# Two of a group's four normalised inputs turned by DMA transposes through DRAM, and the last group's input prepared a slot sooner

## The chip, the cores and the metric

The kernel runs on one core of a Trainium2 chip. The metric is the device time of one execution in microseconds. One execution per kernel is also taken by the hardware profiler, and all views shown here come from such an execution. The engines are called as the profile calls them: PE is the matrix engine and PEld its weight loads, DVE the vector engine, ACT the scalar engine, POOL the GpSimd engine, SP the queue from which this kernel issues all its DMAs.

## The reference

Two layers are applied to `x`, 128 graphs of 128 nodes with 512 features each, in float32.

```
h = relu(layernorm(x));  x = x + norm_adj @ (h @ W0) + b0
h = relu(layernorm(x));  q, k, v = h@Wq+bq, h@Wk+bk, h@Wv+bv        (8 heads of 64)
attn = softmax(q k^T / 8 + (1 - adj) * -1e9);  x = x + (attn @ v) @ Wo + bo
```

`norm_adj` and the mask come from one 128x128 matrix that all graphs share. All the large products are 512x512 weights against 512 rows of a group.

## The kernel before, in words

**Groups and slots.** Four graphs ("elements" 0 to 3) make a group, and there are NG = 32 groups. `xts[g, half]` holds the residual of two elements, 128 nodes by 2 x 512. The program is a sequence of slots t = 0 to 32, and each slot has the stages W, Q, K, V and Y, in this order. W is the first layer's weight product for group t+1, Q, K and V are the projections of group t, and Y is the output projection of group t-1. So a group's first layer runs a slot before its projections, and its output projection is in the same slot, after V.

**Stages and places.** A stage is a 512x512x512 product cut into 2x2 blocks, computed by seven block products instead of eight (class `Projection`, steps n = 0 to 6), and most block products are cut in the same way once more. What a step leaves for later (`tail`) runs in steps 1 and 2 of the stage that follows. All other work is hung on the steps by name: `at(t, "V2", f, ...)` puts a call ahead of step 2 of stage V in slot t, `"V2b"` puts it between the two parts of that step. `block` (L991) walks the steps and calls what the plan holds. The order on each engine is this written order; no scheduler moves anything. "V2" is called a place below.

**Operands.** The left operand of a stage is a tile of 40 slots of 128x128 float32 (class `Operands`). Slots 0 to 15 hold the blocks A11, A12, S1 and A22. The transposed input of elements 0 and 1 goes into A11 and A12 (slots 0 to 7), that of elements 2 and 3 into S1 and A22 (slots 8 to 15). `combine` then makes the sums that the seven products need, four operations over 512 columns and nine over 256, on POOL in most slots. There are three such tiles: `op_mix` (`op_a`, input of W), `op_norm` (`op_h`, input of Q, K and V) and `op_att` (`op_o`, input of Y).

**How the input of Q, K and V is made.** In slot t, for group g = t+1: `ln2` (DVE, then POOL) makes mean and scale, `norm_h` (L662, ACT) writes the normalised element `h` [128 nodes, 512 features], `transpose_h` (L666) turns it by four PE transposes into a small PSUM bank and copies the bank into `op_norm` (L673, ACT). Then `attention_operands` (L675) is the `combine`. `norm_h` stands at V5, V6, Y1 and Y2, `transpose_h` at Y1, Y2, Y3 and Y4, and `attention_operands` at Y5. Q of the next slot reads the result.

**How the softmaxed scores are turned.** These 124 tiles are already turned by DMA. `split_att` (L771) has ACT copy the float32 tile, seen as 16-bit halves, into two planes (all low halves, then all high halves), in a tile of `att_buf` that is free, and SP writes the planes to DRAM. `turn_att` (L777) has SP issue a DMA transpose of the planes back into SBUF, which puts the halves side by side again. `att_buf` has five tiles for the four elements of a group, and `att_of(g, b)` is tile (b - g) mod 5. In slot t these steps belong to group t-1, and `attend` at V0 reads their results; group 31 is turned on PE instead (`transpose_att`).

**The SP queue.** All DMAs stand in one queue in written order, and an entry that waits holds up those behind it. In a slot there are the reloads of the weights (`reload_w`, L966: of each weight four parts, into two buffers in turn, each as soon as the stage that read the buffer is past that part), four plane writes, four DMA transposes, two loads of `x` for group t+2 (`load_x`, at W3 and W5) and two stores of finished halves (`store_half`: one after Y, one at W3). A load of `x` goes into a tile whose store must have landed first. In DVE's order, the statistics of the loaded `x` (`ln1`, at Q0b) stand between reads of PE's banks.

**The end.** In slot 31 there is no W, so the chain that prepares Q and the attention of group 30 has no stage beside it.

Of the kernel before, what the change touches and what calls it, by code (L numbers as in the profile page):

```python
# [9 lines left out]
U16 = mybir.dt.uint16  # L10
# [16 lines left out]
A11, A12, S1, A22, S2, S3, S4 = range(7)  # L27
# [17 lines left out]
LEFT_AT = {A11: 0, A12: 4, S1: 8, A22: 12, S2: 16, S3: 20, S4: 24}  # L45
# [48 lines left out]
def kernel(  # L94
# [16 lines left out]
    nc = tc.nc  # L111
    B, N, D = x.shape
    P = 128
    H = 8
    HD = D // H
    NC = D // P
    GB = 4
    NG = B // GB
# [27 lines left out]


    planes_dram = [dp.tile([P, 2, H * P], U16, tag=f"planes_{b}", name=f"planes_{b}") for b in range(GB)]
    adj_sb, an = (att_buf[2][:, i, :] for i in range(2))
    bias_part = att_buf[4][:, 0:NC, :].rearrange("p c f -> p (c f)")  # L150
    ones = att_buf[4][:, NC, :]
# [430 lines left out]
    hs = {}  # L582
# [82 lines left out]

    def transpose_h(g, b):  # L666
        if b == 0:
            op_h[g] = op_norm
        h2 = hs.pop((g, b))
        pt = small_bank(f"pt_{g}_{b}")  # L670
        for c in range(NC):
            nc.tensor.transpose(pt[:, c * P : (c + 1) * P], h2[:, c * P : (c + 1) * P], ident)  # L672
        nc.scalar.copy(op_h[g].blocks_of(b), pt.rearrange("p (c n) -> p c n", c=NC))  # L673

    def attention_operands(g):  # L675
        op_h[g].combine(nc.vector if g < 2 else nc.gpsimd, g > 0, within=nc.gpsimd)
# [42 lines left out]
    def att_of(g, b):  # L719


        return att_buf[(b - g) % (GB + 1)]
# [65 lines left out]

    def attend(g, b):
        if g not in op_o:  # L790

            op_o[g] = op_mix if g == NG - 1 else op_att
        aT = att_of(g, b if g == NG - 1 else b - 1)
        if b == 2 or b == 3:
            po = small_bank(f"po_{g}_{b}")
        else:
            po = bank["b" if b == 0 else f"a{1 - turn[0]}"]
        for c in range(NC):
            for p in range(2):
                h = 2 * c + p  # L800
                nc.tensor.matmul(  # L801
                    po[p * HD : (p + 1) * HD, c * P : (c + 1) * P],
                    vs[g][:, b, h * HD : (h + 1) * HD],
                    aT[:, p * NC + c, :],
                    start=True,
                    stop=True,
                )
        nc.scalar.copy(op_o[g].blocks_of(b), po.rearrange("p (c n) -> p c n", c=NC))
# [17 lines left out]
    def at(slot, place, f, *args):  # L826
        plan.setdefault((slot, place), []).append((f, *args))

    for t in range(-1, NG + 1):


        last = t == NG - 1
        if 0 <= t - 1 < NG - 1:
            g = t - 1
            for place, first, f, *args in (
                ("Q0", "W1", turn_att, 0),
                ("W1b", "W4b", split_att, 1),
                ("W2", "W5", exponentials, 2, 0, H // 2),
                ("W3", "W6", exponentials, 2, H // 2, H),
                ("W4b", "Q0b", softmax_end, 2),  # L840
                ("W5", "Q1", exponentials, 3, 0, H // 2),
                ("W6", "Q2", exponentials, 3, H // 2, H),
                ("Q2", "Q0", turn_att, 1),
                ("Q0b", "Q2b", softmax_end, 3),
                ("Q3b", "Q4b", split_att, 2),
                ("Q5b", "Q6b", split_att, 3),
                ("K0", "K1", turn_att, 2),
                ("K2", "K3", turn_att, 3),
            ):
                at(t, place if t > 1 else first, f, g, *args)  # L850
            for b in (2, 3, 0, 1):
                at(t, "V0", attend, g, b)
        if t == 0:

            at(0, "Q0b", ln2, 1, 0)
            at(0, "Q1b", ln2, 1, 1)
            at(0, "K6", norm_h, 1, 0)
            at(0, "K6", norm_h, 1, 1)
            at(1, "W0", transpose_h, 1, 0)
            at(1, "W0", norm_h, 1, 2)  # L860
            at(1, "W1", transpose_h, 1, 1)
            at(1, "W1", norm_h, 1, 3)
            at(1, "W2", transpose_h, 1, 2)
            at(1, "W3", transpose_h, 1, 3)
            at(1, "W3", attention_operands, 1)
            at(2, "W6", attention_residual, 1, 0)
            at(2, "W6", attention_residual, 1, 1)
        elif 1 <= t + 1 < NG and t >= 0:
            g = t + 1
            at(t, "K0b", ln2, g, 0)  # L870
            at(t, "K3b", ln2, g, 1)
            at(t, "V5", norm_h, g, 0)
            at(t, "V6", norm_h, g, 1)
            at(t, "Y1", transpose_h, g, 0)
            at(t, "Y1", norm_h, g, 2)
            at(t, "Y2", transpose_h, g, 1)
            at(t, "Y2", norm_h, g, 3)
            at(t, "Y3", transpose_h, g, 2)
            at(t, "Y4", transpose_h, g, 3)
            at(t, "Y5", attention_operands, g)  # L880
            at(t + 1, "Q3", attention_residual, g, 0)
            at(t + 1, "Q4", attention_residual, g, 1)
        if 1 < t <= NG:

            at(t, "Y3" if t == NG else "Q3" if last else "W3", store_half, t - 2, 1)
        if 3 <= t + 2 < NG:
            at(t, "W3" if t > 1 else "W0", load_x, t + 2, (0,))
            at(t, "W5" if t > 1 else "W0", load_x, t + 2, (1,))
        if 2 <= t + 2 < NG:
            g = t + 2  # L890
            at(t, "Q0b", ln1, g, 0, (0,), ())
            at(t, "Q1b", ln1, g, 0, (1,), (0, 1))
            at(t, "Q3b", ln1, g, 1)
            places = (("Q3", "Q5"), ("Q4", "Q6"), ("Q5b", "K1"), ("Q6", "K2"))
            for b, (norm, mix) in enumerate(places):
                at(t, norm, gcn_norm, g, b)
                at(t, mix, gcn_mix, g, b)
            at(t, "K2" if t > 0 else "V1b", gcn_operands, g)
            at(t, "Y1" if t > 0 else "K3", gcn_residual, g, 0)
            at(t, "Y2" if t > 0 else "K3", gcn_residual, g, 1)  # L900
        if 0 <= t < NG:
            g = t
            for b in (0, 1, 3, 2):
                at(t, "V0", scores, g, b)
            if t > 0:
                at(t, "V0", output_operands, t - 1)
            at(t, "V1b", row_max, g, 0)
            at(t, "V3b", exponentials, g, 0, 0, H // 2)
            at(t, "V4b", exponentials, g, 0, H // 2, H)
            at(t, "V6", softmax_end, g, 0)  # L910
            if last:
                at(t, "V5b", row_max, g, 1)
                at(t, "V5b", exponentials, g, 1, 0, H // 2)
                at(t, "V6", exponentials, g, 1, H // 2, H)
                at(t, "Y1b", softmax_end, g, 1)
                at(t, "Y2", transpose_att, g, 0)
                at(t, "Y4", transpose_att, g, 1)
            else:
                if t > 0:
                    at(t, "V3b", row_max, g, 1)  # L920
                    at(t, "Y1", exponentials, g, 1, 0, H // 2)
                    at(t, "Y2", exponentials, g, 1, H // 2, H)
                    at(t, "Y4", softmax_end, g, 1)
                else:
                    at(t, "V4b", row_max, g, 1)
                    at(t, "V5b", exponentials, g, 1, 0, H // 2)
                    at(t, "V6", exponentials, g, 1, H // 2, H)
                    at(t + 1, "W1b", softmax_end, g, 1)
                at(t, "Y3b", split_att, g, 0)
                at(t, "V6b", row_max, g, 2)  # L930
                at(*((t, "Y1") if t > 0 else (1, "W0")), add_mask, g, 3)
                at(*((t, "Y6b") if t > 0 else (1, "W4b")), row_max, g, 3)
        if last:
            g = t
            at(t, "Y0", row_max, g, 2)

            at(t + 1, "W0", combine_w, "o last", nc.gpsimd)
            at(t, "Y1", exponentials, g, 2, 0, H)
            at(t, "Y1b", row_max, g, 3)
            at(t, "Y2b", softmax_end, g, 2)  # L940
            at(t, "Y3", exponentials, g, 3, 0, H)
            at(t, "Y4b", softmax_end, g, 3)
            at(t, "Y6", transpose_att, g, 2)
            at(t + 1, "W0", transpose_att, g, 3)
            for b in range(GB):
                at(t + 1, "W0", attend, g, b)
            at(t + 1, "W0", output_operands, g)

            at(t + 1, "Y4", store_half, g, 0, slice(0, 256))
            at(t + 1, "Y5", store_half, g, 0, slice(256, 512))  # L950
            at(t + 1, "Y6", store_half, g, 1, slice(256, 512))
# [191 lines left out]
```

## Time and profile before

| what | value |
|---|---|
| time, median of 3 runs | 2330.02 us (2326.16 to 2332.68) |
| time of the profiled execution | 2329.11 us |
| its span, first to last instruction | 2327.3 us |
| granted TensorE clock, mean | 0.997 |
| DVE busy | 1869.4 us (80%) |
| ACT busy | 1344.8 us (58%) |
| POOL busy | 1861.7 us (80%) |
| DMA queue, share of 16 engines' span | 74.9% |

Busy times are unions of the instructions' spans on an engine. A slot in the middle takes some 71 us: the scores of V0 start at 1007.11 us in slot 13 and at 1078.46 us in slot 14. The end of slot 13 and the start of slot 14 are used as the example throughout: V0 from 1003.46, the V product from 1010.88 and Y from 1021.88 us in slot 13, W from 1035.06, Q from 1046.77 and K from 1060.65 us in slot 14.

### The profile page before, as it was taken

The numbers are of one execution on the slowest core, as the hardware profiler recorded it, in microseconds if no ns is written. First come the engines' busy times: TensorE is split into PE (matmuls) and PEld (weight loads), VectorE is DVE, ScalarE is ACT, GpSimd is POOL, SyncE is SP. The second block draws the span as 40 slices with busy tenths as digits, with TensorE's granted clock in tenths as the row PEclk, the third lists the DMA queues.
The fourth block names the chain that finished last, engine by engine and source line by source line (L and its number), as shares of the span: only waits on it lengthen the run. The fifth ranks groups of instructions, "written<-read, shape, count | busy, mean of one in ns | idle before, by whom it ended". The sixth has DMA issues, their size and how long they took to land.

```text
span 2327.3 us, 50893 instructions
## 1 busy us (share of the span) xinstructions
PE 2300.2 (99%) x18359; PEld 2155.6 (93%) x18359; DVE 1869.4 (80%) x4832; ACT 1344.8 (58%) x3553; POOL 1861.7 (80%) x1927
## 2 busy tenths in 40 slices
PE   8999999999999999999999999999999999999999
PEld 8889999999999999999999999999999999999988
DVE  6777888788888788887888878888878888888866
ACT  3555665655656556556566565565655665655564
POOL 6898788878788777887778887778877788877764
PEclk9999999999999999999999999999999999999999
DMA  6388877789767788777887678886788877788873
GB/s 199 126 257 247 252 227 232 214 247 276 226 228 217 238 252 248 234 226 216 250 267 225 229 213 249 254 242 227 221 226 257 270 217 230 216 247 259 233 217 104
DMA packets 390764, 536.07 MB, mean 230 GB/s; under 512 B 271856, under 2 KB 279152, under 8 KB 390000
## 3 DMA queue, kind: packets, MB, share of 16 engines
q1 hardware_dynamic: 390512, 532.81, 74.9%
q8 instruction: 146, 2.39, 0.4%
q14 instruction: 106, 0.87, 0.1%
HBM read 358.68 MB, written 109.05 MB: 201 GB/s over the span
## 4 chain that ended last, share of the span: by engine, by line
PE 82%; DMA 5%; DVE 5%; issue 1%; POOL 0%; SPq 0%; ACT 0%; DVEq 0%; ACTq 0%
PE bank_a L387 30%; PE bank_d L387 18%; PE bank_b L387 9%; PE bank_c L387 9%; DMA xt<-in_x_dram 5%; PE pa L604 4%; PE bank_d L734 3%; PE po L801 3%; PE pt L672 2%; DVE xt L428 2%; PE pss L734 1%; DVE xt L438 1%; PE bank_b L801 1%; PE bank_a L801 1%; PE bank_b L734 1%
## 5 line engine op out<-in xcount | busy, mean ns | idle before, releaser
L761 ACT ACTIVATE att<-att,nmx 128x128 f32<-128x128 f32 x1024 | 396.0, 389 | 0.6 <-DVE nmx L753 0.5
L387 PE MATMUL bank_a<-op_h,w 128*128 128x256 f32 x1536 | 364.6, 380 | 0.0
L769 POOL TENSOR_TENSOR att<-att,rsm 128x1024 f32<-128x1024 f32 x128 | 242.8, 1897 | 100.0 <-DVE rsm L768 98.1
L387 PEld LDWEIGHTS bank_a<-op_h,w 128*128 128x128 f32 x1536 | 278.6, 191 | 30.3
L428 DVE TENSOR_TENSOR xt<-xt,bank_d 128x512 f32<-128x512 f32 x732 | 269.1, 416 | 25.9 <-PE bank_d L387 9.0
L332 ACT ACTIVATE h<-xt,nb,rs 128x512 f32<-128x512 f32 x254 | 206.9, 816 | 71.4 <-POOL nb L321 69.7
L319 POOL TENSOR_TENSOR rs<-ve,mhalf 128x2 f32<-128x2 f32 (+1 forms) x129 | 91.3, 708 | 193.3 <-DVE ve L318 193.0
L695 ACT ACTIVATE q<-bank_a,bqk 128x256 f32<-128x256 f32 x192 | 80.6, 470 | 285.7 <-PE bank_a L387 285.7
L774 ACT COPY att<-att 128x2048 uint16<-128x2048 uint16 x124 | 235.4, 1899 | 7.2 <-POOL att L769 7.2
L387 PE MATMUL bank_d<-op_h,w 128*128 128x128 f32 (+1 forms) x1768 | 225.5, 279 | 3.9 <-POOL op_h L90 3.1
L387 PEld LDWEIGHTS bank_d<-op_h,w 128*128 128x128 f32 x1768 | 210.7, 192 | 9.1 <-issue 4.0
L90 POOL TENSOR_TENSOR op_o<-op_o 128x256 f32<-128x256 f32 x297 | 209.3, 729 | 10.0
L90 POOL TENSOR_TENSOR op_h<-op_h 128x256 f32<-128x256 f32 x279 | 196.7, 730 | 13.5 <-DVE op_h L364 3.8
L90 POOL TENSOR_TENSOR op_a<-op_a 128x256 f32<-128x256 f32 x270 | 190.4, 728 | 14.7 <-DVE op_a L364 5.3
L313 DVE BATCH_NORM_STATS2 st<-xt 128x6 f32<-128x512 f32 x256 | 173.2, 676 | 24.8 <-DMA xt<-in_x_dram 24.8
L761 ACT ACTIVATION_READ_ACCUMULATOR att<-att,nmx 128x1 f32 x1024 | 192.8, 188 | 0.0
L438 DVE TENSOR_TENSOR xt<-bank_a,xt 128x512 f32<-128x512 f32 x252 | 167.4, 686 | 18.4 <-PE bank_a L387 10.8
L387 PE MATMUL bank_a<-w,op_o 128*128 128x256 f32 x768 | 181.7, 379 | 0.0
L387 PE MATMUL bank_a<-w,op_h 128*128 128x256 f32 x744 | 179.1, 384 | 0.0
L387 PE MATMUL bank_a<-w,op_a 128*128 128x256 f32 x744 | 176.8, 381 | 0.2 <-DVE xt L438 0.2
L741 DVE SCALAR_TENSOR_TENSOR att<-bank_d,msk 128x512 f32<-128x512 f32 x128 | 82.5, 686 | 104.8 <-PE bank_d L734 96.2
L753 DVE TENSOR_REDUCE nmx<-att 128x8 f32<-128x1024 f32 x128 | 155.0, 1211 | 0.0
(178 smaller groups left out, 5937.8 us busy)
## 6 DMA issues: line engine op xcount, KB each, us to landing
w<-wd_v SPq DMA_DIRECT2D x93, 704.0 KB, 5.6
w<-wd_o SPq DMA_DIRECT2D x93, 704.0 KB, 7.0
planes<-att SPq DMA_DIRECT2D x124, 512.0 KB, 4.5
w<-wd_q SPq DMA_DIRECT2D x90, 704.0 KB, 6.5
w<-wd SPq DMA_DIRECT2D x87, 704.0 KB, 4.2
xt<-in_x_dram SPq DMA_DIRECT2D x63, 512.0 KB, 6.4
out_dram<-xt SPq DMA_DIRECT2D x62, 512.0 KB, 4.4
w<-wd_v SPq DMA_DIRECT2D x31, 448.0 KB, 4.2
```

The source lines that it names most:

```text
L90: engine.tensor_tensor(twice(out), twice(x), twice(y), ALU.subtract if minus else ALU.add)
L313: nc.vector.bn_stats(self.st[:, j, :], self.src[:, j, :])
L332: nc.scalar.activation(h, src[:, j, :], AF.Relu, bias=nb[:, j : j + 1], scale=rs[:, j : j + 1])
L387: nc.tensor.matmul(out, lhsT, rhs, start=start, stop=True, skip_group_check=True)
L428: nc.vector.tensor_tensor(dst, dst, src, f)
L438: nc.vector.tensor_tensor(t, src.rearrange("p (r f) -> p r f", r=2), t, ALU.add)
L734: nc.tensor.matmul(pss[p][:, c, :], qs[g][rows, c, cols], ks[g][rows, c, cols], start=True, stop=True)
L753: nc.vector.tensor_reduce(nmx, att_of(g, b), AX.X, ALU.max, negate=True)
L761: nc.scalar.activation(att[:, h, :], att[:, h, :], AF.Exp, bias=nmx[:, h : h + 1], scale=1.0, accum_out=sm[:, h : h + 1])
L769: nc.gpsimd.tensor_tensor(att, att, rsm.unsqueeze(2).to_broadcast([P, H, P]), ALU.mult)
L774: nc.scalar.copy(planes, halves)
L801: nc.tensor.matmul(po[p * HD : (p + 1) * HD, c * P : (c + 1) * P], vs[g][:, b, h * HD : (h + 1) * HD], aT[:, p * NC + c, :], start=True, s ...
```

## The change

It has two parts.

**Elements 0 and 1 by DMA.** For groups 2 to 30 (29 of 32), elements 0 and 1 are no longer transposed on PE. The new `split_h` has ACT copy the 16-bit halves of `h` into planes, both elements into one tile, and after the second one SP writes that tile (512 KB) to a new DRAM tile `h_dram`. The new `turn_h` has SP issue one DMA transpose from there into slots 0 to 7 of `op_norm`. The tile used for the planes is `att_of(g - 1, -1)`, the fifth of the five, which the scores of the slot don't use. Places change with it: `norm_h` of elements 0 and 1 goes from V5 and V6 to V1 and V2, `split_h` is at V2b and V3, `norm_h` of elements 2 and 3 goes to V5 and V6, `transpose_h` of elements 2 and 3 from Y3 and Y4 to Y1 and Y2, and `turn_h` is at Y0. `attention_operands` stays at Y5.

**The last group a slot sooner.** Group 31 keeps its four PE transposes, but they and what feeds them go from V and Y of slot 30 to Q and K of the same slot, where there is no further group to mix, and the result goes into `op_mix` instead of `op_norm` (so `attend` of group 31 writes to `op_norm`). Its `attention_operands` goes from Y5 to K2. The attention steps of group 30 (`exponentials`, `softmax_end`, `split_att`, `turn_att`) go from W, Q and K of slot 31 to Y of slot 30 and the first steps of Q.

```diff
+    h_dram = dp.tile([P, 2, H * P], U16, tag="planes_h", name="planes_h")
...
     def transpose_h(g, b):
         if b == 0:
-            op_h[g] = op_norm
+            op_h[g] = op_mix if g == NG - 1 else op_norm
...
+    def split_h(g, b):
+        h2 = hs.pop((g, b)).bitcast(U16).rearrange("n (c f z) -> n z c f", c=NC, z=2)
+        planes = att_of(g - 1, -1).bitcast(U16).rearrange("n h k -> n (h k)")
+        nc.scalar.copy(planes.rearrange("n (z c j f) -> n z c j f", z=2, c=NC, j=2)[:, :, :, b, :], h2)
+        if b == 1:
+            nc.sync.dma_start(h_dram, planes.rearrange("n (z f) -> n z f", z=2))
+
+    def turn_h(g):
+        op_h[g] = op_norm
+        blocks = op_norm.t.bitcast(U16)[:, LEFT_AT[A11] : LEFT_AT[A11] + 8, :]
+        nc.sync.dma_start_transpose(out=blocks, in_=h_dram.rearrange("n z f -> (n z) f"))
...
-            op_o[g] = op_mix if g == NG - 1 else op_att
+            op_o[g] = op_norm if g == NG - 1 else op_att
...
-            for place, first, f, *args in (
-                ("Q0", "W1", turn_att, 0),
-                ("W1b", "W4b", split_att, 1),
-                ("W2", "W5", exponentials, 2, 0, H // 2),
...
+            for first, final, place, f, *args in (
+                ("W1", "-Y6", "Q0", turn_att, 0),
+                ("W4b", "-Y6b", "W1b", split_att, 1),
+                ("W5", "-Y3", "W2", exponentials, 2, 0, H // 2),
+                ("W6", "-Y4", "W3", exponentials, 2, H // 2, H),
+                ("Q0b", "-Y5b", "W4b", softmax_end, 2),
+                ("Q1", "-Y5", "W5", exponentials, 3, 0, H // 2),
+                ("Q2", "-Y6", "W6", exponentials, 3, H // 2, H),
+                ("Q0", "Q1", "Q2", turn_att, 1),
+                ("Q2b", "Q0b", "Q0b", softmax_end, 3),
+                ("Q4b", "Q0b", "Q3b", split_att, 2),
+                ("Q6b", "Q2", "Q5b", split_att, 3),
+                ("K1", "Q2", "K0", turn_att, 2),
+                ("K3", "Q5", "K2", turn_att, 3),
             ):
-                at(t, place if t > 1 else first, f, g, *args)
+                place = first if t == 1 else final if last else place
+                at(t - place.startswith("-"), place.strip("-"), f, g, *args)
...
-            at(t, "K0b", ln2, g, 0)
-            at(t, "K3b", ln2, g, 1)
-            at(t, "V5", norm_h, g, 0)
-            at(t, "V6", norm_h, g, 1)
-            at(t, "Y1", transpose_h, g, 0)
...
+            at(t, "K0b" if g < NG - 1 else "Q0b", ln2, g, 0)
+            at(t, "K3b" if g < NG - 1 else "Q3b", ln2, g, 1)
+            if g == NG - 1:
+                places = ("Q3", "Q4", "Q5", "Q5", "Q6", "Q6", "K1", "K2", "K2")
+                steps = ((norm_h, 0), (norm_h, 1), (transpose_h, 0), (norm_h, 2), (transpose_h, 1), (norm_h, 3))
+                steps += ((transpose_h, 2), (transpose_h, 3))
+            else:
+                places = ("V1", "V2", "V2b", "V3", "V5", "V6", "Y1", "Y2", "Y5")
+                steps = ((norm_h, 0), (norm_h, 1), (split_h, 0), (split_h, 1), (norm_h, 2), (norm_h, 3))
+                steps += ((transpose_h, 2), (transpose_h, 3))
+                at(t, "Y0", turn_h, g)
+            for place, (f, b) in zip(places, steps):
+                at(t, place, f, g, b)
+            at(t, places[8], attention_operands, g)
...
-                at(*((t, "Y6b") if t > 0 else (1, "W4b")), row_max, g, 3)
+                at(*((t, "Y3b" if g == NG - 2 else "Y6b") if t > 0 else (1, "W4b")), row_max, g, 3)
```

More of the change, by code (lines that the diff above doesn't have):

```diff
@@ L834 @@
             g = t - 1
-            for place, first, f, *args in (
-                ("Q0", "W1", turn_att, 0),
-                ("W1b", "W4b", split_att, 1),
-                ("W2", "W5", exponentials, 2, 0, H // 2),
[L839 to L848, printed above, removed]
-            ):
-                at(t, place if t > 1 else first, f, g, *args)
+            for first, final, place, f, *args in (
[12 more added lines that the diff above has]
+                ("K3", "Q5", "K2", turn_att, 3),
+            ):
+                place = first if t == 1 else final if last else place
+                at(t - place.startswith("-"), place.strip("-"), f, g, *args)
             for b in (2, 3, 0, 1):
@@ L869 @@
             g = t + 1
-            at(t, "K0b", ln2, g, 0)
-            at(t, "K3b", ln2, g, 1)
-            at(t, "V5", norm_h, g, 0)
-            at(t, "V6", norm_h, g, 1)
-            at(t, "Y1", transpose_h, g, 0)
[L875 to L880, printed above, removed]
+            at(t, "K0b" if g < NG - 1 else "Q0b", ln2, g, 0)
[12 more added lines that the diff above has]
+            at(t, places[8], attention_operands, g)
             at(t + 1, "Q3", attention_residual, g, 0)
```

## The prediction, made before the changed kernel was timed

> **What bounds the kernel.** I read the page's engine shares first, then the waits, the groups, and last the timelines of one slot. The shares and PE's own waits between 200 and 2150 us (two views):
>
> ```profile
> PE 2300.2 (99%) x18359; PEld 2155.6 (93%) x18359; DVE 1869.4 (80%) x4832; ACT 1344.8 (58%) x3553; POOL 1861.7 (80%) x1927
> ```
>
> ```profile
> PE bank_c L387 <- DVE xt L428: 4.0, 9, 1.0
> ```
>
> PE idles about 27 us in 2327 and in the middle almost only in that one place, so PE's instructions are the path and removing some shortens it, as long as nothing else is late. PE's timeline of Y (start, duration):
>
> ```profile
> 1023.61 0.60 PE L672 MATMUL pt<-ident,h 128*128 128x128 f32 x4
> 1024.04 0.61 PE L387 MATMUL bank_c<-w,op_h 128*128 128x128 f32 x4
> ...
> 1029.77 0.60 PE L672 MATMUL pt<-ident,h 128*128 128x128 f32 x4
> 1030.21 0.61 PE L387 MATMUL bank_b<-w,op_o 128*128 128x128 f32 x4
> ```
>
> Four transposes move the next work by 0.43 to 0.44 us, less than the 0.60 shown for them.
>
> The one wait in the middle comes from a DMA. DVE's timeline at the start of Q:
>
> ```profile
> 1048.18 0.20 DVE L768 RECIPROCAL rsm<-sm 128x8 f32<-128x8 f32 x1
> 1049.34 0.70 DVE L313 BATCH_NORM_STATS2 st<-xt 128x6 f32<-128x512 f32 x1 [0.97 <-DMA xt<-in_x_dram]
> 1050.07 0.18 DVE L314 BATCH_NORM_AGGREGATE mv<-st 128x2 f32<-128x6 f32 x1
> 1050.17 0.57 DVE L428 TENSOR_TENSOR xt<-xt,bank_c 128x128 f32<-128x128 f32 x2
> ```
>
> The statistics wait 0.97 us for the loaded x, the read of bank_c stands behind them, and PE's next product into bank_c with it: bank_b starts at 1051.13 where 14 and 2 matmuls after 1048.94 (1.56 and 0.22 us) would have it at 1050.72. So 0.41 of the 0.97 us reached PE and 0.56 was slack. Of such waits there are 20.3 us in 21 between 200 and 2150; less 0.56 each, some 8.5 us reach PE.
>
> **The change, part by part.**
>
> *PE.* 29 groups lose two sets of four transposes: 58 x 0.435 = **25.2 us**. By busy time (76.7 us / 508 = 151 ns each, 232 of them) it would be 35.0, and the sum 2289; I keep the spacing, since the next matmul's start is what the path sees. The Trainium skill (Perfetto Trace Analysis, "Identifying the Most-Contended Engine") calls matmul busy time a bad measure because matmuls are pipelined; by that rule too the busy price is out, and the trace agrees (0.60 shown against 0.44 of spacing).
>
> *ACT.* These groups show what goes and what prices the new copies:
>
> ```profile
> L673 ACT COPY op_h<-pt 128x512 f32<-128x512 f32 x128 | 73.7, 576 | 43.9 <-PE pt L672 43.9
> L774 ACT COPY att<-att 128x2048 uint16<-128x2048 uint16 x124 | 235.4, 1899 | 7.2 <-POOL att L769 7.2
> ```
>
> 58 bank copies of 0.58 go. 58 copies of 128x1024 halves come; no row has this shape. Half of L774 is 0.95; the bounds are 0.58 (the float copy with half the elements) and 1.90 (L774 whole, as if the interleaved output doubled it). I take 0.95, the same kind of operation. ACT's total grows by some 21 us on 58%; what matters is place. In V, ACT has this (pauses in brackets):
>
> ```profile
> 1012.91 0.59 ACT L709 COPY v<-bank_a 128x512 f32<-128x512 f32 x1 [1.69 <-PE bank_a L387]
> 1013.80 0.59 ACT L709 COPY v<-bank_d 128x512 f32<-128x512 f32 x1 [0.30 <-PE bank_d L387]
> 1017.09 0.59 ACT L709 COPY v<-bank_a 128x512 f32<-128x512 f32 x1 [2.71 <-PE bank_a L387]
> ```
>
> From 1013.40 (the first copy occupies 0.49, start to start) come: norm 0.72 to 1014.12 (the bank_d copy now 0.32 late; the DVE add behind it then pauses 0.08 instead of 0.40 before its next read, so PE sees nothing), copy 0.49, norm 0.72, two splits of 0.90 (L774 takes 1.80 start to start): 1017.13. The third copy is 0.04 late. Cost 0; the cover is the 2.71 us pause. With 1.80 a split, the third copy would end 1.84 us late, at 1019.52; PE's third product on bank_a starts at 1019.03, so 0.5 us a slot, 14 us in all. In Y, ACT loses two norms and two copies, some 2.4 us, and split_att of element 0 leaves earlier.
>
> *SP and DMA.* Per slot one plane write and one transpose are added, of the size of those that exist: 2.9 us at best from issue to landing for the write, 4.1 to 11.5 (median 6.6) for the transpose, which holds the queue 1.7 to 8.3 us. In the trace's packet records a transpose is 2048 packets of 24.65 ns over 16 engines, 3.2 us, and a write 1.4, together **4.6 us of DMA time a slot**. SP's timeline of the end of slot 13, and then the windows of that stretch (bounds, length, busy time of PE, PEld, DVE, ACT and POOL, then PEclk, DMA share and GB/s):
>
> ```profile
> 1014.47 12.76 SPq L971 DMA_DIRECT2D w<-wd  x4
> 1032.10 0.34 SPq L775 DMA_DIRECT2D planes<-att  x1
> ```
>
> ```profile
> 1009.00:1015.00 6.00, 6.00 (x65) 5.67 (x62) 4.62 (x7) 2.26 (x4) 5.69 (x6) 1.00 0.00 0
> 1018.00:1021.00 3.00, 3.00 (x22) 2.79 (x22) 2.86 (x9) 3.00 (x16) 2.66 (x4) 1.00 0.02 5
> 1021.00:1027.00 6.00, 6.00 (x49) 5.75 (x48) 5.37 (x13) 4.53 (x14) 5.08 (x3) 1.00 0.67 240
> 1027.00:1030.00 3.00, 3.00 (x22) 2.75 (x22) 2.26 (x8) 3.00 (x12) 3.00 (x2) 1.00 0.46 153
> 1030.00:1033.00 3.00, 3.00 (x26) 2.92 (x25) 2.49 (x7) 2.77 (x4) 2.93 (x3) 1.00 0.03 14
> 1033.00:1050.00 17.00, 17.00 (x118) 15.91 (x117) 15.36 (x39) 8.75 (x35) 14.56 (x15) 1.00 0.92 312
> ```
>
> DMA is idle for 2.9 us in 1018 to 1021 and for 2.0 + 1.6 + 2.9 in 1021 to 1033, then nearly full. The write is issued at 1017.2 and lands near 1020.2; behind it waits the first weight reload (1014.47 before), 3 us late, for W at 1035. turn_h waits for that landing (slots 0 to 7 were last read at V2) and issues near 1020.2. With the DMA quiet it holds SP some 2 us and lands at 1024.3 to 1027. Behind it stand three reloads, issued before at 1020.96, 1021.37 and 1026.91; the first two move 1 to 1.5 us. Of 9.4 us idle, 4.6 are used, so the DMAs that start at 1032 find the engines free as before: cost 0. If that cover fails, it is rival 2. POOL's combine takes the turned blocks at 1032.71 (L361), and PE needs its results at 1048.9 while it ends at 1044.67, so turn_h has 5 us before POOL waits and over 8 before PE does.
>
> *DVE.* It loses nothing. In Y it waits for PE before several reads (in DVE's timeline 0.47 us at 1027.81, 0.23 at 1029.97, 0.29 at 1031.75), so it can follow PE forward by the 0.87 us.
>
> *Last group.* In slot 31:
>
> ```profile
> 2245.61 0.61 PE L387 MATMUL bank_d<-op_h,w 128*128 128x128 f32 x4
> 2249.30 2.76 PE L387 MATMUL bank_d<-op_h,w 128*128 128x128 f32 x10 [3.09 <-POOL op_h L90]
> ```
>
> From 2245.61 to the bank_a group at 2253.48 are 7.87 us; a slot earlier the same (2189.54 to 2192.22) took 2.68. POOL's combine comes too late there; it moves to K2 of slot 30, where POOL has a pause of 6.63 us before 2216.26 and 12 us of work (ending near 2216.5, 0.3 late for the next combine, which PE needs at 2232.9). The four transposes only move. DVE also waited there for ACT's exponentials (2.92 us); they move into Y of slot 30, where ACT has shed its norms and copies. So **5.2 us** go, bounds 0 (another wait in Q) and 5.2.
>
> *Sum.* 2329.1 - 25.2 - 5.2 = 2298.7 for the profiled execution. The median shown lies 0.9 above it, so **2299 us**. Unknown: the x waits, from -8.5 (all gone, if the loads gain on PE) to about +10 (0.35 us more a slot, since PE arrives sooner at a load that may not).
>
> **Rivals.**
>
> 1. *ACT in V is too full* (splits of 1.9 us). +14: 2313. For it: no row has this output pattern; against: L774 reads with the same stride.
> 2. *Slower: the x loads slip.* The transpose pushes the reloads, these push planes, stores and x in the full stretch from 1033. PE then gains nothing in Q and waits: 3.2 us later, less the half us of slack, is 2.7 x 29 = 78, so 2299 + 78 = 2377. It decides once the load comes more than about 1.0 us later relative to PE (30.4 / 29). For it: the chain to PE is real today, and DMA share is 0.92 to 1.09 from 1033 on; against: 9.4 us idle just ahead. The Trainium skill (VectorE: DVE Perf Modes, "Rules for kernel authors") advises TensorE for a full 128x128 transpose wherever PSUM will do as its target, which speaks for this rival; it weighs the transpose by itself, and here PE has no idle time to give. By its 1309 ns for a 128x128 block of 16-bit values by DMA, the sixteen blocks of one turn_h would take 20.9 us one after another (an estimate) and miss the combine at 1032.71; the existing transposes' 4.1 to 11.5 us from issue to landing say otherwise, and the measurement decides.
> 3. *DVE doesn't follow.* DVE is busy 11.20 of W's 11.71 us. If it gains nothing in Y, PE pays the 0.87 us back in bank_c's wait each slot and only the last group's 5.2 remain: 2325, within the noise. Against: the pauses in Y.
>
> **Chances.** Forecast 0.77 (2288 to 2309), rival 1 0.08, rival 2 0.09, rival 3 0.06. About 0.3% (7 us) can be told from no change. Faster is the forecast and rival 1, 0.85; same rival 3, 0.06; slower rival 2, 0.09. The range goes from 2288 to rival 1 with 1 us over it, 2314.
>
> **What would show it.** Right: 232 PE transposes of h fewer; slots of some 70.5 us; DVE's x waits not above 20 us in the middle; no wait of POOL's combine for the turned planes; the 3.09 us ahead of bank_d gone. Wrong: ACT's third copy in V over a us later (rival 1); longer waits of the statistics for x and more than 4 us of PE waiting for DVE (rival 2); such waits of up to 0.9 us in all slots with x in time (rival 3). The forecast falls if slots stay at 71 us or more.

## The result, and the profile after

| | before | after |
|---|---|---|
| median | 2328.94 us (2326.16 to 2332.68, 4 runs) | 2300.92 us (2299.26 to 2302.29, 4 runs) |
| profiled execution | 2329.11 us | 2300.24 us |
| its span | 2327.3 us | 2298.4 us |

The ratio is 0.9871 (95% interval 0.9859 to 0.9883): faster by 1.3%. The forecast was 2299 us. The total hides two terms that were off in opposite directions, and they show only when the saving is split by slot. Measured from the first score matmul of one slot to that of the next:

| stretch | before | after | difference |
|---|---|---|---|
| 27 slots, 2 to 28: the shortest slot | 70.83 | 70.06 | -0.77 each, -20.8 |
| the same slots: sum above 27 x the shortest | 11.5 | 9.0 | -2.5 |
| the slot before these | 78.11 | 76.73 | -1.4 |
| the last two | 67.83 + 60.75 | 68.72 + 55.49 | -4.4 |
| ahead, slot 0 and tail | | | +0.2 |

Together -28.9 us, as between the profiled executions. The shortest slots are those in which PE waits for no load, and they repeat to 0.02 us. What lies above them is mostly pauses of PE behind loads of x, which differ from one execution to the next. Of the -1.4 in the slot before these nothing can be put down to the change beyond its 0.77: the kernel with the last group's part alone takes 76.26 us there, and a second run of a variant below 80.20.

The engine shares of the changed kernel, and PE's and DVE's waits between 200 and 2130 us (total, times, longest):

```profile
PE 2274.9 (99%) x18127; PEld 2131.8 (93%) x18127; DVE 1863.2 (81%) x4832; ACT 1366.8 (59%) x3553; POOL 1862.8 (81%) x1927
```

```profile
PE bank_c L388 <- DVE xt L429: 3.0, 9, 0.6
```

```profile
DVE st L314 <- DMA xt<-in_x_dram: 16.2, 18, 1.4
```

232 matmuls are gone (18359 to 18127). PE is still the path at 99%, and the waits for x fell from 20.3 us in 21 to 16.2 in 18. In the example, the statistics at the start of Q, which waited 0.97 us before, do not wait in this execution (DVE's timeline; no bracket stands behind the start):

```profile
1037.25 0.64 DVE L314 BATCH_NORM_STATS2 st<-xt 128x6 f32<-128x512 f32 x1
1037.93 0.18 DVE L315 BATCH_NORM_AGGREGATE mv<-st 128x2 f32<-128x6 f32 x1
1038.11 0.61 DVE L429 TENSOR_TENSOR xt<-xt,bank_c 128x128 f32<-128x128 f32 x2
```

PE's timeline in Y of the same slot 13 (its scores start at 996.84; they did at 1007.11 before), and DVE's beside it:

```profile
1015.79 0.60 PE L674 MATMUL pt<-ident,h 128*128 128x128 f32 x4
1016.22 0.39 PE L388 MATMUL bank_c<-w,op_h 128*128 128x128 f32 x2
1016.45 1.06 PE L388 MATMUL bank_b<-w,op_o 128*128 128x128 f32 x8
1017.34 1.89 PE L388 MATMUL bank_a<-w,op_o 128*128 128x256 f32 x8
1019.07 0.61 PE L388 MATMUL bank_b<-w,op_o 128*128 128x128 f32 x4
1019.53 1.83 PE L388 MATMUL bank_d<-w,op_o 128*128 128x128 f32 x14
```

```profile
1017.54 0.88 DVE L429 TENSOR_TENSOR xt<-xt,bank_b 128x256 f32<-128x256 f32 x2 [0.47 <-PE bank_b L388]
1018.34 1.14 DVE L429 TENSOR_TENSOR xt<-xt,bank_d 128x128 f32<-128x128 f32 x4
```

The same read and product before (DVE's timeline, then PE's):

```profile
1027.81 0.88 DVE L428 TENSOR_TENSOR xt<-xt,bank_b 128x256 f32<-128x256 f32 x2 [0.47 <-PE bank_b L387]
1028.60 1.14 DVE L428 TENSOR_TENSOR xt<-xt,bank_d 128x128 f32<-128x128 f32 x4
```

```profile
1030.66 1.73 PE L387 MATMUL bank_d<-w,op_o 128*128 128x128 f32 x14
```

Ahead of the bank_a group at 1017.34 and of the bank_b group at 1019.07 stood four transposes each before (at 1027.61 and 1029.77 there); both places are empty now. The product into bank_d starts at 1019.53, 0.05 us after DVE's last read of that bank ends (1018.34 + 1.14 = 1019.48). Before, that read ended at 1029.74 and the product started at 1030.66: 0.9 us of slack. PE's timeline marks no wait here, since the product starts within 0.02 us of its usual time; but the weight load of the first bank_d matmul, which before started 0.11 us ahead of that matmul, beside the one before it, starts only at 1019.52, that matmul lasts 0.38 us instead of 0.28, and the next groups come 0.10 us late. This is the candidate for the term that the prediction missed; a run below tests it.

ACT's groups (busy, mean ns, idle before), and its timeline in V:

```profile
L790 ACT COPY att<-att 128x2048 uint16<-128x2048 uint16 x124 | 234.9, 1895 | 60.5 <-POOL att L785 60.5
L682 ACT COPY att<-h 128x1024 uint16<-128x1024 uint16 x58 | 57.5, 1042 | 0.0
L675 ACT COPY op_h<-pt 128x512 f32<-128x512 f32 x66 | 38.7, 586 | 51.8 <-PE pt L674 51.8
```

```profile
1002.64 0.59 ACT L725 COPY v<-bank_a 128x512 f32<-128x512 f32 x1 [1.69 <-PE bank_a L388]
1003.12 0.82 ACT L333 ACTIVATE h<-xt,nb,rs 128x512 f32<-128x512 f32 x1
1003.84 0.57 ACT L725 COPY v<-bank_d 128x512 f32<-128x512 f32 x1
1004.31 0.82 ACT L333 ACTIVATE h<-xt,nb,rs 128x512 f32<-128x512 f32 x1
1005.02 1.98 ACT L682 COPY att<-h 128x1024 uint16<-128x1024 uint16 x2
1006.91 0.59 ACT L725 COPY v<-bank_a 128x512 f32<-128x512 f32 x1
```

A split occupies 0.95 us from start to start (1.89 for two). The pause of 2.71 us ahead of the third copy is used up to the last tenth: it starts 10.07 us after the scores, 0.09 later than before (9.98).

SP's queue and the DMA windows of the end of slot 13 (columns as above: length, busy time of PE, PEld, DVE, ACT, POOL, then PEclk, DMA share, GB/s):

```profile
1007.08 0.34 SPq L684 DMA_DIRECT2D planes_h<-att  x1
1007.51 0.38 SPq L992 DMA_DIRECT2D w<-wd  x1
1010.10 2.31 SPq L689 DMA_TRANSPOSE op_h<-planes_h  x1
1012.51 4.46 SPq L992 DMA_DIRECT2D w<-wd  x3
1020.37 0.34 SPq L791 DMA_DIRECT2D planes<-att  x1
```

```profile
1006.00:1009.00 3.00, 3.00 (x24) 2.84 (x23) 2.96 (x8) 3.00 (x12) 2.92 (x5) 1.00 0.40 150
1009.00:1012.00 3.00, 3.00 (x20) 2.79 (x19) 2.75 (x9) 2.79 (x12) 1.87 (x4) 1.00 0.97 285
1012.00:1018.00 6.00, 6.00 (x47) 5.69 (x47) 5.01 (x11) 4.49 (x18) 6.00 (x3) 1.00 1.08 311
1018.00:1021.00 3.00, 3.00 (x23) 2.83 (x22) 2.90 (x10) 2.34 (x5) 3.00 (x3) 1.00 0.46 166
1024.00:1040.00 16.00, 16.00 (x113) 15.05 (x113) 15.18 (x41) 8.16 (x37) 13.82 (x15) 1.00 0.96 325
```

turn_h is issued when the write has landed, 3.0 us after it, and holds SP for 2.31 us. The DMA engines are full from 1009 to 1018, where the same stretch before (1019 to 1028) had shares of 0.02 to 0.67; then they have a lull of 3 us (0.46) and are full again from 1021 (0.95), in the stretch that carries the loads of x. Seen from the scores of its slot, the first load of x still lands 0.9 us earlier than before (41.18 instead of 42.09 us, medians of slots 3 to 28).

Slot 31, PE's timeline at the start of Q, where the 3.09 us wait for POOL was:

```profile
2218.24 1.89 PE L388 MATMUL bank_a<-op_a,w 128*128 128x256 f32 x8
2220.61 0.71 PE L388 MATMUL bank_c<-w,op_o 128*128 128x128 f32 x4 [0.47 <-DVE xt L429]
2221.16 1.73 PE L388 MATMUL bank_d<-op_a,w 128*128 128x128 f32 x14
...
2226.86 1.80 PE L388 MATMUL bank_d<-op_a,w 128*128 128x128 f32 x14 [0.39 <-ACT q L711]
```

The wait for POOL is gone, and two short ones, for DVE and for ACT, are new.

### The profile page after: what moved, and what is told of

Its sections match the earlier page's. It is cut to its first block, busy times and chain, and to the rows that moved or that the text cites. A ratio compares the mean times of both kernels' runs of the same rounds, so it can differ in the third digit from the quotient of the medians.

```text
span 2298.4 us, 50576 instructions
## 1 busy us (share of the span) xinstructions
PE 2274.9 (99%) x18127; PEld 2131.8 (93%) x18127; DVE 1863.2 (81%) x4832; ACT 1366.8 (59%) x3553; POOL 1862.8 (81%) x1927
## 4 chain that ended last, share of the span: by engine, by line
PE 74%; POOL 6%; DMA 6%; DVE 3%; issue 2%; ACT 2%; SPq 0%; POOLq 0%; DVEq 0%; ACTq 0%
PE bank_a L388 27%; PE bank_d L388 16%; PE bank_c L388 8%; PE bank_b L388 8%; PE pa L605 4%; DMA xt<-in_x_dram 4%; PE bank_d L750 3%; PE po L816 3%; POOL xt L337 2%; DVE xt L429 2%; PE pss L750 1%; PE bank_b L816 1%; PE bank_a L816 1%; PE bank_b L750 1%; POOL att L765 1%
## 5 line engine op out<-in xcount | busy, mean ns | idle before, releaser
L388 PE MATMUL bank_a<-op_h,w 128*128 128x256 f32 x1488 | 353.3, 380 | 0.0
L388 PEld LDWEIGHTS bank_a<-op_h,w 128*128 128x128 f32 x1488 | 270.0, 191 | 29.4
L388 PE MATMUL bank_d<-op_h,w 128*128 128x128 f32 (+1 forms) x1712 | 216.9, 278 | 0.7 <-issue 0.3
L90 POOL TENSOR_TENSOR op_a<-op_a 128x256 f32<-128x256 f32 x279 | 197.1, 730 | 14.9 <-DVE op_a L365 5.3
L388 PEld LDWEIGHTS bank_d<-op_h,w 128*128 128x128 f32 x1712 | 203.1, 192 | 5.0 <-issue 3.4
L90 POOL TENSOR_TENSOR op_h<-op_h 128x256 f32<-128x256 f32 x270 | 190.7, 731 | 13.1 <-DVE op_h L365 3.8
L314 DVE BATCH_NORM_STATS2 st<-xt 128x6 f32<-128x512 f32 x256 | 172.9, 675 | 20.3 <-DMA xt<-in_x_dram 20.0
L439 DVE TENSOR_TENSOR xt<-bank_a,xt 128x512 f32<-128x512 f32 x252 | 166.9, 684 | 11.5 <-PE bank_a L388 3.9
```

The lines of the kernel that those rows point to most:

```text
L90: engine.tensor_tensor(twice(out), twice(x), twice(y), ALU.subtract if minus else ALU.add)
L314: nc.vector.bn_stats(self.st[:, j, :], self.src[:, j, :])
L388: nc.tensor.matmul(out, lhsT, rhs, start=start, stop=True, skip_group_check=True)
L439: nc.vector.tensor_tensor(t, src.rearrange("p (r f) -> p r f", r=2), t, ALU.add)
```

## The experiments

All kernels were timed against the kernel before; ratios are to it, with 95% intervals. Diffs are against the changed kernel.

**The two parts alone.** Elements 0 and 1 by DMA, with the last group as before (group 31's places, the attention of group 30 and the operand tiles put back):

```diff
-            op_h[g] = op_mix if g == NG - 1 else op_norm
+            op_h[g] = op_norm
...
-                places = ("Q3", "Q4", "Q5", "Q5", "Q6", "Q6", "K1", "K2", "K2")
+                places = ("V5", "V6", "Y1", "Y1", "Y2", "Y2", "Y3", "Y4", "Y5")
```

> The DMA part alone: elements 0 and 1 of groups 2 to 30 by DMA, the last group and the attention of group 30 as before the change. My theory from the two traces: of the 28.9 us that the span lost, the last group gave 3.5 and the DMA part 25.4, so this kernel has a span of about 2302 us and a time near 2304, 1.1% below before, and the 3.09 us wait for op_h in slot 31 is back. By the prediction's own terms the last group gave 5.2: 2304 of span and 2306. Rival: the two parts help each other (slots follow one another without a break), then this one is over 2308.

Measured 2303.65 us, 0.989 (0.9873 to 0.9907); span 2302.1. The shortest slots take 70.05 us, and the last two 127.95 with the wait for POOL in them.

The last group sooner, with four PE transposes in all other groups:

```diff
-                places = ("V1", "V2", "V2b", "V3", "V5", "V6", "Y1", "Y2", "Y5")
-                steps = ((norm_h, 0), (norm_h, 1), (split_h, 0), (split_h, 1), (norm_h, 2), (norm_h, 3))
+                places = ("V5", "V6", "Y1", "Y1", "Y2", "Y2", "Y3", "Y4", "Y5")
+                steps = ((norm_h, 0), (norm_h, 1), (transpose_h, 0), (norm_h, 2), (transpose_h, 1), (norm_h, 3))
...
-                at(t, "Y0", turn_h, g)
```

> The last group alone: groups 2 to 30 are transposed on PE as before the change, group 31 and the attention of group 30 as after it. My theory: 3.5 us below before (2325.5 where before has 2329), the wait for op_h in slot 31 gone and three smaller ones of 0.4 to 0.6 us (PE's weight loads for DVE's read of bank_c, for DVE's add to v, for ACT's copy of q) in its place. By the prediction's term 5.2 us: 2324. Slots in the middle as before, 70.83 us where nothing waits.

Measured 2324.93 us, 0.9975 (0.9962 to 0.9988); the shortest slots are 70.81 us and the last two 124.94 instead of 128.58 (-3.64). The time alone could not tell 3.5 from 5.2; the last two slots do. The two ratios multiply to 0.9865, against 0.9871 for the change: the parts add. The 0.77 us a slot belong to the DMA part, the last slots to the other.

**Is the missing 0.1 us the bank_d read?** One of the two remaining transposes goes back from Y2 to Y4, ahead of the bank_b group, where it gives DVE 0.44 us. Its work on PE is the same.

```diff
-                places = ("V1", "V2", "V2b", "V3", "V5", "V6", "Y1", "Y2", "Y5")
+                places = ("V1", "V2", "V2b", "V3", "V5", "V6", "Y1", "Y4", "Y5")
```

> The changed kernel with the PE transpose of element 3 at Y4 instead of Y2, nothing else. The theory: in Y the PE now reaches its second product on bank_d 0.10 us before DVE has finished reading bank_d, since both removed sets stood between that read and the product; with one of them back at Y4 and one less at Y2 the read comes 0.44 us earlier and the product where it was relative to it. Then the shortest slots fall from 70.06 to 69.96 us, the wait of PE's weight load at bank_d is gone, and the time falls by 29 x 0.10 = 2.9 us. Rival: the 0.10 us come from elsewhere (a slower matmul after the moved place, DMA writes into the same tile): shortest slots stay at 70.06 and the time within 1 us of the changed kernel.

Measured 2295.73 us, 0.9855 (0.9838 to 0.9872). The shortest slots fall from 70.06 to 69.94 us. PE's and DVE's timelines in this kernel:

```profile
1017.02 0.60 PE L674 MATMUL pt<-ident,h 128*128 128x128 f32 x4
1017.45 0.61 PE L388 MATMUL bank_b<-w,op_o 128*128 128x128 f32 x4
1017.90 1.73 PE L388 MATMUL bank_d<-w,op_o 128*128 128x128 f32 x14
```

```profile
1016.28 1.14 DVE L429 TENSOR_TENSOR xt<-xt,bank_d 128x128 f32<-128x128 f32 x4
```

The read ends at 1017.42, 0.48 us ahead of the product, whose 14 matmuls take 1.73 us instead of 1.83. The weight load at the product again starts 0.11 us ahead of it. The same number of instructions, in another order, gives the 0.11 us back. So the product did wait for that read.

To see the two versions side by side, both ran again on one chip:

> The changed kernel as it is, once more, so that it and c_again are measured side by side: 0.987 of before, shortest slots 70.06 us.

> c_y1_y4 once more, side by side with the changed kernel: if the 0.11 us a slot that its trace showed are all, it is 3.2 us below the changed kernel (0.9857 of before against 0.987); if the waits for x, which differ from run to run, made part of its first result, the difference is under 2 us or over 5.

Measured 2302.13 us, 0.9877 (0.9859 to 0.9895), for the change and 2296.26 us, 0.9851 (0.9835 to 0.9867), for the moved transpose: 5.9 us apart, with intervals that overlap. By the expectation a difference over 5 us means that waits for x made part of it. The two profiled executions are only 0.8 us apart: the shorter slot gives 3.2 us (29 x 0.11) and the pauses above it 2.6 (8.8 to 6.2 us), but the slot before these takes 3.9 us more (80.20 against 76.31) and the stretch ahead of it 1.0. So the 3.2 us are the moved transpose; whether it causes anything beyond them was not separated.

**The new waits of the last slot.** With the transpose at Y4, the splits of elements 2 and 3 of group 30 go behind Q's bank copies on ACT:

```diff
-                ("Q4b", "Q0b", "Q3b", split_att, 2),
-                ("Q6b", "Q2", "Q5b", split_att, 3),
-                ("K1", "Q2", "K0", turn_att, 2),
-                ("K3", "Q5", "K2", turn_att, 3),
+                ("Q4b", "Q3b", "Q3b", split_att, 2),
+                ("Q6b", "Q5b", "Q5b", split_att, 3),
+                ("K1", "K0", "K0", turn_att, 2),
+                ("K3", "K2", "K2", turn_att, 3),
```

> As c_y1_y4, and in slot 31 the two plane copies of elements 2 and 3 of group 30 and their DMA transposes go back to the places of the other slots (Q3b, Q5b, K0, K2), so that ACT's copies of q in Q are not behind them. Theory: the 0.6 us that PE's weight load waited for ACT's copy of q are gone, 0.5 us below c_y1_y4, in all 3.4 below the changed kernel. Rival: PE then waits elsewhere (turned tiles too late for V0, DVE's reads): no gain over c_y1_y4, or a loss of a us or more.

Measured 2294.69 us, 0.985 (0.9834 to 0.9867). The last slot takes 54.69 us instead of 55.47, and PE's wait for ACT's q is gone from its waits. So 0.8 us of the shortfall were those splits, 1.9 us each, ahead of the copies. The wait of 0.5 us for DVE's read of bank_c stays; what the rest of the shortfall is was not tested. This version has the lowest median of all, though it can't be told from the one before it by the time alone.

**Is the DMA cover real, and what if it goes?** A further DMA of the same 512 KB, from DRAM to DRAM, whose result nothing reads: once in the lull (Y0, behind turn_h), once in the full stretch (W1).

```diff
+    def copy_h():
+        nc.sync.dma_start(h_copy, h_dram)
...
+                at(t, "Y0", copy_h)
```

> The changed kernel with one DMA more per slot for groups 2 to 30: a copy of the planes (512 KB) from DRAM to DRAM, issued at Y0 right behind the DMA transpose of h. It leads nowhere; it only takes DMA time in the stretch in which the engines have pauses. The theory (the DMA part is free because 9.4 us of DMA pauses lie in the end of V and in Y, and the loads of x in W are what PE depends on): 4.6 of the 9.4 us are used, so up to some 4 us more fit and the time stays within 3 us of the changed kernel. Rival (no real cover; each us of DMA work slips to the loads of x): statistics wait for x by the copy's time more, 1.5 to 3 us a slot, PE by 1 to 2.5, and the time rises by 30 to 70 us.

```diff
+                at(t + 1, "W1", copy_h)
```

> The same extra copy from DRAM to DRAM, issued at W1 of the next slot, where the DMA engines are already full, ahead of the loads of x. The theory: the load of x lands later by the copy's own time (1.5 to 3 us), the statistics wait that much longer, and beyond some 0.56 us of slack PE waits one for one: 28 slots x 1 to 2.5 us, 28 to 70 us above the changed kernel, most of it as waits of PE for DVE's read of bank_c. Rival (the loads of x do not set PE's pauses): within 5 us of the changed kernel.

In the lull: 2305.73 us, 0.9898 (0.9883 to 0.9913). The shortest slots stay at 70.07, and slots 2 to 28 together take 4.8 us more than in the change. In the full stretch: 2326.73 us, 0.9982 (0.997 to 0.9994), the whole gain of the transposes lost. PE's and DVE's waits in the second, each from its own view:

```profile
PE bank_c L389 <- DVE xt L430: 21.2, 20, 2.2
```

```profile
DVE st L315 <- DMA xt<-in_x_dram: 43.3, 28, 3.0
```

DVE waits for x in 28 slots (16.2 us in 18 in the change), and PE behind it. Both lie somewhat outside what was expected (within 3 us, and 28 to 70). The same transfer costs 5 us in one place and 26 in the other; the lull nearly covers one more plain copy, and the chain from x through DVE to PE is what rival 2 said.

**Is there room for all four elements?** Elements 2 and 3 by DMA too, with a second write (V6b) and a second transpose (Y2), and no transposes on PE in these groups:

```diff
+                steps += ((split_h, 2), (split_h, 3))
+                at(t, "Y0", turn_h, g, 0)
+                at(t, "Y2", turn_h, g, 1)
```

> All four elements of groups 2 to 30 by DMA: elements 2 and 3 are split into planes at V6 by ACT, written to a second DRAM tile and turned by a second DMA transpose at Y2 into slots 8 to 15; PE makes no transpose of h in these groups. PE sheds 0.87 us more a slot, 25 us in all. The DMA work added per slot is 9.2 us, about all of the 9.4 us of pauses that the prediction counted. Theory: the second write and transpose come late (write near the end of V, landing in Y), push the reloads into W and with them the load of x by some 2 us, so that PE waits more than the 0.87 us it gains; also the combine on POOL starts later. I expect between 2295 and 2340, most likely 2310, slower than the changed kernel. Rival (the cover is wide enough): 2276.

Measured 2453.42 us, 1.053 (1.0506 to 1.0554). The first transpose stood behind the second write in SP's queue and was issued 5.0 us later than in the change (18.30 instead of 13.33 us after the scores, medians), so the order was changed (first transpose at V5, second write at Y1b, second transpose at Y2b):

```diff
+                at(t, "V5", turn_h, g, 0)
+                at(t, "Y1b", write_h, g, 1)
+                at(t, "Y2b", turn_h, g, 1)
```

> All four elements by DMA as in f_all_four, in a better order of the SP queue: the first transpose (slots 0 to 7) goes to V5, so that it does not stand behind the second write, and the second write and transpose go to Y1b and Y2b behind two of the three reloads. In f_all_four the first transpose was issued 4.7 us later than in the changed kernel and the second landed 8 us after its issue. Theory: the DMA time of 4.6 us a slot more is what counts; it no longer fits ahead of W, the load of x still comes 2 to 4 us late, and the kernel is slower than the changed one, 2310 to 2380. Rival (f_all_four was slow by its queue order alone): about 2276.

Measured 2422.33 us, 1.0395 (1.0373 to 1.0417), still above the range expected. PE's waits in it:

```profile
PE bank_c L389 <- DVE xt L430: 93.8, 25, 5.9
```

The load of x lands 3.0 us later after the scores than in the change (44.16 instead of 41.18), within the 2 to 4 that were expected. Removing two more sets from PE would save some 25 us, and PE now waits nearly four times that. The rest of the loss, which the expectation had left out, is for the most part the clock: 95.6 us between 200 and 2280 run at a granted clock of 0.50 (none in the change), by an estimate 48 us of work lost (half of them). Neither order of two pairs fits the lull. Whether the DMA engines' time or the order of the queue makes the loads late is not settled: SP itself waits 177 us in this run for the second write to land, and in the example the DMA share is only 0.25 from 997 to 1000, while the queue is held by that wait.

**How full is ACT in V?** Each split copy is made twice, the second time with the same values:

```diff
-        nc.scalar.copy(planes.rearrange(...)[:, :, :, b, :], h2)
+        for _ in range(2):
+            nc.scalar.copy(planes.rearrange(...)[:, :, :, b, :], h2)
```

> The changed kernel in which ACT makes each copy into the planes of h twice (the second writes the same values again). This gives ACT in V what rival 1 of the prediction had feared, two splits of about 1.9 us each instead of 0.99. By that rival's working PE's third product on bank_a waits 0.5 us a slot, 14 us in all; the write of the planes also starts 2 us later. If ACT's pause in V covers more than I thought, the time stays within 3 us; if the late planes also reach POOL's combine, over 25 us.

Measured 2334.39 us, 1.0023 (1.0013 to 1.0033). ACT's timeline and then PE's:

```profile
1019.51 4.14 ACT L683 COPY att<-h 128x1024 uint16<-128x1024 uint16 x4
1023.56 0.58 ACT L726 COPY v<-bank_a 128x512 f32<-128x512 f32 x1
```

```profile
1021.62 1.80 PE L388 MATMUL bank_d<-w,op_h 128*128 128x128 f32 x14
1024.19 1.99 PE L388 MATMUL bank_a<-w,op_h 128*128 128x256 f32 x8 [0.77 <-ACT v L726]
```

Four splits occupy 4.05 us, 2.16 more than two. The third copy ends at 1024.14, and the product into bank_a starts right behind it. The shortest slots are 71.27 us, 1.20 above the change: 0.93 ahead of this product, 0.10 in its first matmul and 0.17 later. ACT's pause was used up, and 2.16 us more of ACT's time a slot lost more than the change had gained. POOL's combine does not wait for the late planes here either.

## Why the prediction was right, and where it was not

The time, 2300.92 against 2299, and the likeliest case were right, and so were the signs that it named: 232 matmuls fewer, slots of 70.4 us on average, 16.2 us of waits for x, no 3.09 us ahead of bank_d. That the time came within 2 us is in part luck, since the errors of its terms partly cancel. By its steps:

- **PE, 25.2 us: the price right, the sum 2.9 too high.** In a slot without pauses, each removed set takes 0.437 us out of PE's sequence. But 0.10 a slot comes back, so 29 slots gave 0.77 each, 22.3 us.
- **DVE: the step that failed.** "It can follow PE forward by the 0.87 us" was argued from DVE's pauses in Y. The read that mattered is the one of bank_d at 1028.60. The pause of 0.47 us ahead of it waits for a group of bank_b that PE computes ahead of both removed sets, so it could not shrink (it is 0.47 us at 1017.54 too), and the other two pauses come behind the read. Its 0.9 us of slack towards the next product was the two sets of transposes (0.87 us). So rival 3's mechanism, at another bank than it named, was true to 0.10 of its 0.87 us, and the moved transpose shows it.
- **Last group, 5.2 us: measured 3.6 by the last two slots** (3.64 alone; 3.74 between the DMA part alone and the whole change). The wait for POOL went as told. The working took the whole of the old stretch as gain and didn't ask what the moved work meets: `row_max` of element 3 (1.21 us on DVE, at 2214.20) now stands among the reads of Y, and two splits stand before q's copies on ACT. Only the splits were tested (0.8 us). The bound (0 to 5.2, "another wait in Q") held it.
- **The x waits, taken as 0 in -8.5 to +10: about -3.** In slots 2 to 28, 2.5 us fewer pauses, and some 0.6 in the slot before them (1.4 less 0.77), which lies within what differs between executions there. The loads kept up while PE came sooner. 22.3 + 3.6 + 3.1 - 0.2 gives the 28.8 measured: two terms too high by 4.5 together, one too low by 3.
- **ACT, cost 0: right.** 0.95 us a split was priced and 0.95 measured from start to start; the third copy is 0.09 us late instead of 0.04. Rival 1 would have cost more than its 14 us. Its 0.5 us a slot was the delay at the first product alone; the run with doubled splits, whose copy came 0.4 us later than in that case, lost 0.93 there and 0.27 behind it. By that, the rival's own case is an estimated 0.75 us a slot, 22 us.
- **SP and DMA, cost 0: right.** The write lands 2.96 us after its issue (2.9), turn_h holds SP 2.31 (2) and lands 4.36 after its issue (4.1 to 6.8). The next two reloads, issued 13.85 and 14.26 us after the scores before, come at 15.67 and 16.29: 1.8 and 2.0 later, not 1 to 1.5. POOL's combine does not wait. From the 1309 ns that the Trainium skill gives for one 128x128 block by DMA (VectorE: DVE Perf Modes, "The three transpose paths"), sixteen blocks one after another were an estimated 20.9 us; issue to landing of the 29 transposes is 4.1 to 6.7 us, so the blocks do not follow one another at that price.
- **Rival 2** was the right thing to fear. Its price was 2.7 us a slot for a slip of 3.2; the copy in the full stretch raised DVE's waits for x by 27 us and the time by 26. It needed a transfer in the wrong place or a second pair, and the change had neither.

## What to carry to other kernels

When work is taken off the bounding engine, ask for each of its products which read must have ended before it, and how much of that slack the removed work was; pauses elsewhere on the reading engine say nothing about it. What remains can be placed where it restores that slack at no cost. A transfer is hidden by a lull at its own place in the slot: the same 512 KB cost 5 us in 29 slots beside one stage and 26 us beside the next, while the mean DMA share of the two kernels was 82% and 81%.

## What the hardware showed that was not expected

A long wait of PE costs more than its length. In the second kernel with all four elements by DMA, these windows surround a wait of DVE for x of 5.55 us (PEclk is the third figure from the end):

```profile
1016.00:1018.00 2.00, 0.00 (x0) 0.00 (x0) 0.00 (x0) 0.00 (x0) 2.00 (x2) 1.00 0.70 281
1018.00:1020.00 2.00, 0.11 (x1) 0.11 (x1) 1.50 (x5) 0.00 (x0) 0.52 (x1) 0.80 0.75 220
1020.00:1022.00 2.00, 2.00 (x10) 2.00 (x11) 1.45 (x5) 0.00 (x0) 0.96 (x3) 0.50 1.05 404
...
1024.00:1026.00 2.00, 2.00 (x7) 1.64 (x6) 1.91 (x6) 0.16 (x1) 0.55 (x1) 0.50 1.18 232
1026.00:1028.00 2.00, 2.00 (x20) 2.00 (x19) 1.32 (x4) 2.00 (x3) 1.64 (x4) 0.99 0.99 334
```

PE stood for 4.71 us and then ran at half clock until about 1026. The last group before shows the same after its 3.09 us: granted clock 0.50 between 2250 and 2252 and 0.77 in the two microseconds after, in all 3.4 us at half clock, by an estimate 1.7 of the 2.1 us by which the stretch was longer than its wait (5.2 against 3.1). The Trainium skill describes it (TensorE: Matmul & The Clock Gate, "HAM oscillation — how this bites in real kernels"): its rule is to leave PE no idle gap over about 3.4 us, since the clock is halved after one. The traces agree for the long waits, but show no such limit: the clock fell after the 3.09 us here, and in the first kernel with all four elements it stayed at 1.00 after a wait of 3.61 us (at 428). The pauses of up to 0.6 us in the changed kernel's middle leave the clock at 1.00 in every window shown, so the many short waits for x cost nothing by the clock.
